# Gates fetched to half of the partitions and copied to the other half by ScalarE

## The chip, the core and the metric

The kernel runs on one core of a Trainium2 chip. A core has five engines with a queue of instructions each: TensorE (PE in the profile, its weight loads PEld), VectorE (DVE), ScalarE (ACT), GpSimd (POOL) and SyncE (SP), which here only issues DMAs. Each engine works through its queue in order, and engines wait for one another and for DMAs by semaphores. The metric is the device time of one execution in microseconds; the figure to compare with is the median of the runs.

## What is computed

The input x is 2 images of 128 channels and 256 x 256 pixels. One layer follows: window attention with a halo (on the four pixel parities apart, because of a fixed mask) after a normalization over channels, and then a mixture of experts in which each pixel takes the two best of eight experts. Cut to what matters:

```python
x = x + attention(_ln_c(x), W_qkv, W_out, rel_height, rel_width)
t = _to_tokens(x)                                   # one token per pixel, 128 channels
h = _ln_t(t)
router_probs = softmax(h @ router_w + router_b)     # 8 experts
top_p, top_i = top_k(router_probs, 2)
top_p = top_p / sum(top_p)
expert_out = einsum('bnd,edc->bnec', h, expert_w) + expert_b
t = t + einsum('bnk,bnkc->bnc', top_p, expert_out[top_i])
```

All of it is in float32.

## The kernel before

**Tiles and loops.** Channels lie on the 128 partitions. The image is cut into 64 strips of 8 pixel rows (32 per image). Each strip has four planes, one for each parity of pixel row and column, so the main loop (L980) runs over 256 planes n. In one pass it does the attention of plane n, the projections (queries, keys, values, relative positions) of plane n + 1, the statistics and the routing of earlier row pairs, and the experts of a row pair (512 tokens: 128 channels x 512) of the strip before.

**Order.** The order within a pass is written out by hand (`manual_schedule`, L979): each generator (`scores`, `attend`, `out_project`, `project`, `norms`, `route`) is moved on by `next(...)` at the place where its instructions shall stand in the queues of all engines. TensorE's order in a usual plane is: scores (L437, L454), values and projections of the next plane (L310, L369, L383, L408), four expert products of the row pair before (L677, experts 4, 6, 7, 5), sums and attended values (L475, L485), statistics (L543), expert products 0, 1, 2, the output projection (L513), expert product 3.

**Gates.** A row pair goes through these steps, spread over three planes:
1. `norms` squares the rows on ScalarE (L537), sums over channels on TensorE (L543), transposes on VectorE (L552) and makes the rate 1/sqrt(variance) in `rstd`: VectorE L192 to L195, then Ln and Exp on ScalarE (L196, L197), then VectorE L198, L199, L559, L561.
2. In the next plane `route` (L576 to L608) picks the two best experts on VectorE, with an Exp on ScalarE (L581). `spread` transposes the gates (L614) and writes them to a DRAM buffer gd (L622).
3. In the same plane they are read back, each of them as one row of 512 numbers that is repeated on all 128 partitions: the rate rb for the attention's normalization (`fetch_rstd`, L628), the mean term sb (`fetch_means`, L657) and the eight gates gb (`fetch`, L652). `to_all` (L631) builds the repeated source. A gate's buffer is one of eight; a write of a single column by VectorE (L651) or ScalarE (L649) just ahead of the DMA marks the place in the order from which the DMA may start.
4. In the plane after that, `means` (L662) adds the mean term and `times` (L668) multiplies the rows by each gate, experts 0 to 4 and 6 on VectorE, 5 and 7 on GpSimd; `product` (L677) multiplies by the expert's weights, and `end` (L683) adds the sum to the rows, which are then stored (L715). `ln1` (L236, GpSimd) applies rb.

**SyncE's queue.** In a usual plane it issues, in this order: gates 5 and 7, gd twice, the value rows to DRAM (vrows, L329), rb, sb, the value windows from DRAM (vwin twice, L341, which need the value rows landed), gates 0, 1, 2, the load of x (L117), gate 3, the store (L715), gates 4 and 6.

**Blocks of instructions.** TensorE's instructions are fetched in blocks of 256. `addr_align` pads its stream so that what follows stands at a given slot of a block: once at the start (L101), at the start of each usual plane (L995, slot 157), and in planes without a normalization ahead (plane 6 and planes 250 to 255) before the sums (L1027, slot `SUMS_AT`).

**The end.** `finish_last` (L722) handles the last row pairs: those called row B here (the `nxt` of the loop's end, L793) and then five more, one of which (f) is routed first and the last four in one pass over VectorE (L798 to L849). Their gates are fetched whole (L745, L747), multiplied in `multiply` (L760, two of eight on GpSimd in the first four) and summed in `products` (L767) into the four quarters of one PSUM tile, accs; L878 and L882 add.

Of the kernel before, what the change touches and what calls it, by code (L numbers as in the profile page):

```python
# [11 lines left out]
F32 = mybir.dt.float32  # L12
AF = mybir.ActivationFunctionType
ALU = mybir.AluOpType
# [3 lines left out]
P = 128  # L18
HEADS, DH = 4, 32
E = 8  # L20
# [23 lines left out]
KR, KC = 6, 10  # L44
NK = KR * KC
SLOT = 64
BLOCK, FIRST_LIMIT, SUMS_AT = 256, 99, 40
NU = 9
FILL = 6

# [2 lines left out]
def kernel(  # L53
# [16 lines left out]
    nc = tc.nc  # L70
# [7 lines left out]
    CH = 2 * W  # L78
    NT = CH // P
# [13 lines left out]
    def mm_tile(name):  # L93
        return ps_mm.tile([P, 512], F32, tag="mm", name=name)

    def ctile(shape, name):
        return const.tile(shape, F32, tag=name, name=name)


    nc.scalar.preload_act_table_set("natural_log_exp_and_others")  # L100
    nc.tensor.addr_align(BLOCK, offset=51, max_nops=0)  # L101


    strips = [(b, s) for b in range(B) for s in range(NS)]
# [27 lines left out]
    rb = ctile([P, E], "rb")  # L132
    ew = ctile([P, E, P], "ew")
# [491 lines left out]
    def fetch_rstd(gd, nm):  # L625

        rb = gates.tile([P, NT * P], F32, tag="rb", name=f"rb{nm}", bufs=2)
        nc.sync.dma_start(rb, to_all(gd, E + 1))  # L628
        return rb

    def to_all(gd, j):  # L631

        return gd[j * NT : (j + 1) * NT].rearrange("r k -> (r k)").partition_broadcast(P)

    class Experts:

# [6 lines left out]
        def fetch(self, e, eng):  # L643


            nm = "_".join(str(v) for v in (*self.at, e))
            self.gb[e] = gates.tile([P, NT * P], F32, tag="gb", name=f"gb{nm}", bufs=8)
            if eng is nc.scalar:
                eng.copy(self.gb[e][:, 0:1], onesm[:, 0:1])  # L649
            else:  # L650
                eng.memset(self.gb[e][:, 0:1], 0.0)  # L651
            nc.sync.dma_start(self.gb[e], to_all(self.gd, e))  # L652

        def fetch_means(self):

            self.sb = gates.tile([P, NT * P], F32, tag="sb", name="sb%d_%d" % self.at, bufs=1)
            nc.sync.dma_start(self.sb, to_all(self.gd, E))  # L657

        def means(self):

# [24 lines left out]

    class NoExperts:
        def fetch(self, e, eng):
            pass

        def fetch_means(self):  # L690
# [31 lines left out]
    def finish_last(ex, nxt, gated):  # L722
# [27 lines left out]
        def multiply(at, row):  # L750

            sb, gb = rooms.pop(0)
            src = rows_of(*at)
            xs = work.tile([P, CH], F32, tag="o", name=f"xl{row}")
            nc.vector.tensor_add(xs, src, sb)
            out = []
            for e in range(E):
                xe = work.tile([P, CH], F32, tag="xe", name=f"xel{row}_{e}", bufs=8)
                eng = nc.gpsimd if e in (2, 5) and row < 4 else nc.vector
                eng.tensor_tensor(xe, xs, gb[e], ALU.mult)  # L760
                out.append(xe)
            return out

        def products(acc, xes):
            order = (0, 1, 3, 2, 4, 6, 5, 7)
            for j, e in enumerate(order):
                nc.tensor.matmul(  # L767
                    acc, lhsT=ew[:, e, :], rhs=xes[e], start=(j == 0), stop=(j == E - 1)
                )

        gd = spread(f, None, made[0], "_c")
# [18 lines left out]
        nxt.means()  # L790
        ex.end()
        for e in (0, 1, 2, 3, 4, 6, 5, 7):
            nxt.times(e, nc.gpsimd)  # L793
        for e in (0, 1, 2, 3, 4, 6, 5, 7):
            nxt.product(e)

# [66 lines left out]
            2, gds[1], [gates.tile([P, CH], F32, tag="gb", name=f"gl2_{e}", bufs=8) for e in range(E)]  # L863
        )

        accs = ps_att.tile([P, 4, CH], F32, tag="att", name="accs")
        todo = [f] + rows
        before = nxt
        for row, at in enumerate(todo):
            xes = multiply(at, row)  # L870
            if row < 2:
                fetch_all(row + 3, gds[row + 2])
            if row == 0:
                before.end()
                store(*to_store.pop())
            else:
                src = rows_of(*todo[row - 1])
                nc.vector.tensor_add(src, accs[:, (row - 1) % 4], src)  # L878
                store(*todo[row - 1])
            products(accs[:, row % 4], xes)  # L880
        src = rows_of(*todo[-1])
        nc.vector.tensor_add(src, accs[:, (len(todo) - 1) % 4], src)  # L882
        store(*todo[-1])

    n_planes = 4 * len(strips)
# [1 line left out]
    def row_at(n):  # L887

        i, pl = divmod(n + 2, 4)
        for j, k in ((i + 1, pl + 2), (i + 2, pl - 2)):
            if 0 < j < len(strips) and k in ln_rows(j) and (k > 1 or strips[j][1] == 0):
                return j, k
        return None
# [77 lines left out]
    none = iter(())  # L973
    gated, ex, nxt = None, NoExperts(), NoExperts()
    last = ctile([P, 1], "last")
    pool, dve = nc.gpsimd, nc.vector

    ET = mybir.EngineType
    with tc.manual_schedule(engines={ET.PE, ET.DVE, ET.Activation, ET.Pool, ET.SP}):  # L979
        for n in range(n_planes):  # L980
            i, pl = divmod(n, 4)
            score, attn, outp, ahead, norm, rout = none, none, none, none, none, none
            if n < n_planes:
                score = scores(n, states[n])
                attn = attend(n, states[n])
                outp = out_project(n, states[n])
            if n + 1 < n_planes:
                states[n + 1] = {}
                ahead = project(n + 1, states[n + 1])

            usual = n > 6 and row_at(n - 1) is not None
            if usual:
                nc.tensor.addr_align(BLOCK, offset=BLOCK - FIRST_LIMIT)  # L995


            next(score, None)
            new, row = NoExperts(), None
            if gated and gated[0]:  # L1000
                rout = route(*gated[0], *gated[2])
            next(rout, None)
            nxt.fetch(5, nc.scalar)
            for _ in rout:
                pass
            next(score, None)
            next(ahead, None)
            nxt.fetch(7, nc.scalar)
            if gated:
                f, c, made = gated  # L1010
                gd = spread(f, c, made[0], f"_{n}")
                new = Experts(*f, gd) if f else new
            if n + 1 < n_planes:
                send_values(n + 1, states[n + 1]["sent"])
            if gated and c:
                row = (*c, fetch_rstd(gd, f"_{n}"))
            next(ahead, None)
            if n + 1 < n_planes:
                states[n + 1]["shift"]()
            filling = n < FILL  # L1020
            if not filling:
                next(ahead, None)
                next(ahead, None)
            for e in (4, 6, 7, 5):
                ex.product(e)
            if n >= 6 and not usual:
                nc.tensor.addr_align(BLOCK, offset=SUMS_AT)  # L1027


            f = (i - 1, pl) if 0 < i <= len(strips) else None  # L1030
            c = row_at(n)
            if f or c:
                room = None
                if filling:
                    room = ps_acc.tile([P, 512], F32, tag="acc", name=f"plt_{n}")
                norm = norms(f, c, f"_{n}", room)
            next(norm, None)
            next(attn, None)
            nxt.means()
            new.fetch_means()  # L1040
            if n + 1 < n_planes:
                take_values(n + 1)
            for e in (0, 1, 2, 3):
                nxt.times(e, dve)
            new.fetch(0, dve)
            for e in (4, 6):
                nxt.times(e, dve)
            new.fetch(1, dve)
            ex.end()
            new.fetch(2, dve)  # L1050
            next(attn, None)
            next(attn, None)


            ex = nxt
            next(norm, None)
            if filling:
                next(ahead, None)
                next(ahead, None)
            load_x((n + 9) // 4, (n + 9) % 4, paced=True)  # L1060
            new.fetch(3, dve)
            while to_store:
                store(*to_store.pop())
            next(ahead, None)
            ex.product(0)
            made = next(norm, None)
            ex.product(1)
            ex.product(2)
            new.fetch(4, nc.scalar)
            nxt.behind(6)  # L1070
            nxt.times(5, pool)
            if row:
                ln1(*row, pool)
            if pl == 3 and i + 2 < len(strips):
                halo(i + 2)
            nxt.times(7, pool)
            if n + 2 < n_planes:
                borders(n + 2)
            next(outp, None)
            ex.product(3)  # L1080
            next(outp, None)
            new.fetch(6, dve)
            gated, nxt = (f, c, made) if made else None, new
            states.pop(n, None)

        finish_last(ex, nxt, gated)
# [59 lines left out]
```

## Time and profile before

| | |
|---|---|
| three runs | 4287.52, 4296.25, 4299.03 us (median 4296.25) |
| the profiled execution | 4302.19 us, its span 4300.4 us |
| mean granted clock of TensorE | 0.994 |
| moved by DMA | 1022 MB, of it 12.6 MB instructions in 769 packets |
| share of the 16 DMA engines, data queue | 75.7% |
| gates fetched | 2008 DMAs of 256 KB, 5.7 us to landing (median) |
| value windows fetched | 512 DMAs of 240 KB, 4.8 us |
| expert products L677 | 4016 TensorE matmuls, 1880.8 us |
| products by gates L668 | VectorE 1500, 685 ns each; GpSimd 508, 1272 ns each |
| usual plane, start to start | 16.25 us |
| from the last plane's start to the end | 92.4 us |

How to read it: the profile gives each engine's busy time and, for each group of instructions, the line, the engine, the operation, the tiles (out<-in), the shape and the count; then the busy time, the mean time of one and the idle time of the engine ahead of it with what ended that idle time. SPq marks DMA issues by SyncE; a DMA's time to landing runs from its issue to its semaphore. In a timeline line the first number is the start and the second the length, in microseconds, of the instructions merged into that line.

### The profile page before, as it was taken

To read this page: it belongs to the slowest core of one execution; us is meant where nothing else is said; L and a number is where in the kernel's file an instruction comes from. 1 tells how busy PE (TensorE), PEld (TensorE's weight loads), DVE (VectorE), ACT (ScalarE), POOL (GpSimd) and SP (SyncE) were. 2 spreads that over 40 slices of the span, in tenths; PEclk is the share of its full clock that TensorE was granted. 3 is DMA by queue.
4 is the path that set the end of the run, shared out by engine and by line. 5 is a ranking of instruction groups with operands and counts; after the bars stand their busy time and mean duration, and the time that the engine had idled before them with its cause. 6 is when DMAs were issued, how large, how long until landed. Compare 5 with 4: busy or idle time off the path is not lost.

```text
span 4300.4 us, 224047 instructions
## 1 busy us (share of the span) xinstructions
PE 4214.7 (98%) x94273; PEld 2457.6 (57%) x94273; DVE 3786.3 (88%) x11752; ACT 1315.5 (31%) x3750; POOL 1093.2 (25%) x1125
## 2 busy tenths in 40 slices
PE   7999999999999999999999999999999999999997
PEld 5555555555555555555555555555555555555553
DVE  5888898998988888998898888989898888888887
ACT  3333333332323232333333333323233333333320
POOL 1222222222222222222222222222222222222222
PEclk9999999999999999999999999999999999999999
DMA  4777777877787877887778787787778787777776
GB/s 141 228 248 238 245 242 244 244 245 243 240 248 233 251 235 234 247 244 242 247 239 249 237 249 239 246 245 244 238 243 249 234 249 238 243 234 247 232 217 198
DMA packets 824576, 1022.15 MB, mean 238 GB/s; under 512 B 137634, under 2 KB 409634, under 8 KB 823594
## 3 DMA queue, kind: packets, MB, share of 16 engines
q1 hardware_dynamic: 822864, 1007.52, 75.7%
q8 instruction: 769, 12.60, 1.3%
q14 instruction: 213, 1.74, 0.1%
q10 hardware_dynamic: 730, 0.29, 0.0%
HBM read 863.78 MB, written 143.75 MB: 234 GB/s over the span
## 4 chain that ended last, share of the span: by engine, by line
PE 97%; issue 1%; DVE 1%; DMA 1%; SPq 0%; ACT 0%; POOL 0%; POOLq 0%; DVEq 0%
PE acc L677 41%; PE att L454 8%; PE att L485 7%; PE pv L310 7%; PE plt L543 6%; PE pu L369 5%; PE po L513 5%; PE pk L383 5%; PE pq L408 5%; PE att L437 4%; PE att L475 3%; DMA gl<-gd_l 1%; PE accs L767 0%; PE pltn L253 0%; DMA xt<-in_x_dram 0%
## 5 line engine op out<-in xcount | busy, mean ns | idle before, releaser
L677 PE MATMUL acc<-xe,ew 128*128 128x512 f32 x4016 | 1880.8, 599 | 10.2 <-issue 8.9
L677 PEld LDWEIGHTS acc<-xe,ew 128*128 128x128 f32 x4016 | 740.9, 190 | 913.0 <-issue 856.3
L668 DVE TENSOR_TENSOR xe<-xs,gb 128x512 f32<-128x512 f32 x1500 | 927.6, 685 | 8.6
L672 POOL COPY last<-xe 128x1 f32<-128x1 f32 x250 | 45.9, 184 | 3042.7 <-DVE gb L651 3042.7
L668 POOL TENSOR_TENSOR xe<-xs,gb 128x512 f32<-128x512 f32 x508 | 645.4, 1272 | 12.2 <-DMA gb<-gd 10.7
L454 PE MATMUL att<-qs,kcol 32*60 32x32 f32 x32768 | 393.9, 222 | 25.2 <-issue 24.7
L454 PEld LDWEIGHTS att<-qs,kcol 32*60 32x60 f32 x32768 | 388.1, 126 | 29.7 <-issue 29.0
L236 POOL TENSOR_TENSOR xn<-xt,rb 128x512 f32<-128x512 f32 x249 | 374.4, 1504 | 87.5 <-DMA rb<-gd 74.2
L485 PEld LDWEIGHTS att<-pT,vwin 64*32 64x32 f32 x32768 | 350.8, 105 | 48.6 <-issue 11.1
L485 PE MATMUL att<-pT,vwin 64*32 64x32 f32 x32768 | 348.7, 201 | 9.1 <-issue 8.4
L462 ACT ACTIVATE pT<-att 128x1024 f32<-128x1024 f32 x256 | 262.0, 1023 | 269.4 <-PE att L454 269.3
L310 PE MATMUL pv<-wt,xn 128*128 128x128 f32 x2048 | 300.3, 290 | 0.0
L537 ACT ACTIVATE sq<-xt 128x512 f32<-128x512 f32 x501 | 290.2, 630 | 0.0
L357 DVE STREAM_TRANSPOSE au<-auT 128x512 f32<-128x512 f32 x256 | 269.5, 1053 | 8.8
L373 DVE STREAM_TRANSPOSE uT<-pu 128x512 f32<-128x512 f32 x256 | 183.2, 716 | 105.2 <-PE pu L369 102.1
L394 ACT COPY kcol<-pk 128x560 f32<-128x560 f32 (+2 forms) x344 | 183.0, 532 | 290.5 <-PE pk L383 287.7
L513 PE MATMUL po<-o,wt 128*128 128x512 f32 x512 | 262.1, 593 | 4.5 <-ACT kcol L404 2.1
L369 PE MATMUL pu<-xn,wrel 128*128 128x512 f32 x512 | 266.0, 601 | 0.0
L408 PE MATMUL pq<-xn,wt 128*128 128x512 f32 x512 | 261.8, 592 | 1.6 <-issue 1.6
L383 PE MATMUL pk<-xn,wt 128*128 128x512 f32 (+2 forms) x528 | 262.4, 580 | 0.0
L310 PEld LDWEIGHTS pv<-wt,xn 128*128 128x128 f32 x2048 | 251.0, 193 | 10.6 <-DVE xn L236 0.2
L437 PEld LDWEIGHTS att<-au,keys 32*64 32x64 f32 x8192 | 116.0, 131 | 195.5 <-PE po L513 189.2
(2445 smaller groups left out, 4935.1 us busy)
## 6 DMA issues: line engine op xcount, KB each, us to landing
gb<-gd SPq DMA_DIRECT2D x2008, 256.0 KB, 5.7
vwin<-vrows SPq DMA_DIRECT2D x512, 240.0 KB, 4.8
xt<-in_x_dram SPq DMA_DIRECT2D x256, 256.0 KB, 6.6
out_dram<-xt SPq DMA_DIRECT2D x256, 256.0 KB, 6.0
sb<-gd SPq DMA_DIRECT2D x251, 256.0 KB, 4.3
rb<-gd SPq DMA_DIRECT2D x249, 256.0 KB, 3.5
vrows<-vr SPq DMA_DIRECT2D x168, 256.0 KB, 3.9
vrows<-vr SPq DMA_DIRECT2D x160, 128.0 KB, 3.4
```

The lines of the kernel that those rows point to most:

```text
L236: eng.tensor_tensor(xn[i % 2][:, :, :, k, 1 : PC + 1], ln1_src(i, k).rearrange("p (y j x) -> p y x j", y=2, x=2), rb.rearrange("p (y j x) ...
L310: nc.tensor.matmul(pv[:, j * P : (j + 1) * P], lhsT=xp[:, k, 1 : PC + 1], rhs=wv, start=True, stop=True,)
L369: nc.tensor.matmul(pu, lhsT=wrel, rhs=inner, start=True, stop=True)
L383: nc.tensor.matmul(pk[:, : m * PC], lhsT=wk, rhs=xp[:, part[0] : part[0] + m, 1 : PC + 1], start=True, stop=True,)
L408: nc.tensor.matmul(pq, lhsT=wq, rhs=inner, start=True, stop=True)
L437: nc.tensor.matmul(sc[rows, h].rearrange("p (t w z) -> p t w z", w=2, z=16)[:, :, w], lhsT=keys[hp, turn, w], rhs=au[hp, half * NP + w : ( ...
L454: nc.tensor.matmul(sc[rows, h, 32 * t : 32 * t + 32], lhsT=kk[hp, half * HP + t, 0:NK], rhs=qs[hp, m0 : m0 + 2].rearrange("p m a s -> p (m ...
L485: nc.tensor.matmul(av[hp, half, 32 * t : 32 * t + 32], lhsT=vv[rows, t, hp], rhs=pT[rows, h, 32 * t : 32 * t + 32], start=True, stop=True,)
L513: nc.tensor.matmul(po, lhsT=wo, rhs=state["o"].rearrange("p f z -> p (f z)"), start=True, stop=True)
L537: nc.scalar.activation(sq, src, AF.Square)
L668: eng.tensor_tensor(self.xe[e], self.xs, self.gb.pop(e), ALU.mult)
L677: nc.tensor.matmul(self.acc, lhsT=ew[:, e, :], rhs=self.xe.pop(e), start=(e == 0), stop=not self.xe)
```

## The change

Gates, means and rates are fetched to partitions 0 to 63 alone (`fetch_half`). ScalarE copies them to partitions 64 to 127 (`other_half`, called by `double`, `double_means` and for the rates directly). The copies stand at these places of ScalarE's queue: gate 3 after the values' copy of the next plane, gates 4, 6 and 5 after the projections' copies, then, behind a copy of one column that waits for the attended values (`behind_values`), the rates, the means, gate 7 and the new gate 0, all ahead of the Ln of `norms`; and gates 1 and 2 after its Exp and after the mark of gate 4. The slots of two alignments change. In `finish_last` row B's products and all products of the five later row pairs go to VectorE in expert order, and each later row pair has a PSUM tile of its own from the pool of three. The places of the DMA issues in SyncE's queue stay.

```diff
-BLOCK, FIRST_LIMIT, SUMS_AT = 256, 99, 40
+BLOCK, FIRST_LIMIT, SUMS_AT = 256, 99, 9
...
-    nc.tensor.addr_align(BLOCK, offset=51, max_nops=0)
+    nc.tensor.addr_align(BLOCK, offset=23, max_nops=0)
...
-        nc.sync.dma_start(rb, to_all(gd, E + 1))
+        fetch_half(rb, gd, E + 1)
...
+    def fetch_half(tile_, gd, j):
+        nc.sync.dma_start(tile_[0:SLOT], to_all(gd, j, SLOT))
+    def other_half(tile_):
+        nc.scalar.copy(tile_[SLOT:], tile_[0:SLOT])
...
-            nc.sync.dma_start(self.gb[e], to_all(self.gd, e))
+            fetch_half(self.gb[e], self.gd, e)
+        def double(self, e):
+            other_half(self.gb[e])
...
-                eng = nc.gpsimd if e in (2, 5) and row < 4 else nc.vector
-                eng.tensor_tensor(xe, xs, gb[e], ALU.mult)
+                nc.vector.tensor_tensor(xe, xs, gb[e], ALU.mult)
...
         for e in (0, 1, 2, 3, 4, 6, 5, 7):
-            nxt.times(e, nc.gpsimd)
+            if e > 2:
+                nxt.double(e)
+            nxt.times(e, nc.vector)
...
-        accs = ps_att.tile([P, 4, CH], F32, tag="att", name="accs")
+        accs = []
...
-            products(accs[:, row % 4], xes)
+            accs.append(mm_tile(f"accl{row}"))
+            products(accs[row], xes)
...
             nxt.fetch(7, nc.scalar)
+            nxt.double(3)
...
             c = row_at(n)
+            for e in (4, 6, 5):
+                nxt.double(e)
...
             new.fetch(3, dve)
+            nc.scalar.copy(behind_values, states[n]["att"][:, 1, 511:512])
+            if row:
+                other_half(row[2])
+            new.double_means()
+            nxt.double(7)
+            new.double(0)
...
             made = next(norm, None)
             ex.product(1)
             ex.product(2)
             new.fetch(4, nc.scalar)
+            new.double(1)
+            new.double(2)
```

## The prediction

> **What bounds the kernel now.** I read the engine shares first, then the chain of work that ended last.
>
> ```profile
> PE 4214.7 (98%) x94273; PEld 2457.6 (57%) x94273; DVE 3786.3 (88%) x11752; ACT 1315.5 (31%) x3750; POOL 1093.2 (25%) x1125
> ...
> PE 97%; issue 1%; DVE 1%; DMA 1%; SPq 0%; ACT 0%; POOL 0%; POOLq 0%; DVEq 0%
> ```
>
> TensorE is the bound, and VectorE at 88% is close behind; ScalarE has room. In the timeline a plane starts with the first matmul of L437. Plane 8 starts at 139.58 us and plane 250 at 4124.05, so 242 planes take 3984.5 us; the usual plane is 16.246, and 242 of those are 3931.5. So 53 us are lost in the loop. The waits of TensorE between 300 and 4100 us say where:
>
> ```profile
> PE att L454 <- issue: 16.7, 29, 1.4
> PE acc L677 <- issue: 8.9, 20, 0.8
> ```
>
> L485 adds 3.3. No engine releases these. In the timeline they sit after the 98th, 354th and 610th of a plane's 736 TensorE instructions, 256 apart, where a 16 KB packet of the instruction queue brings the next block. Nothing else holds TensorE in the loop: a gain there can only come out of these 53 us.
>
> Next, one plane of the timeline, from ScalarE's Ln (L196) to the Ln of the plane after it at 2029.03:
>
> ```profile
> 2012.78 0.18 ACT L196 ACTIVATE r__121_38773<-plg 128x8 f32<-128x8 f32 x1 [7.12 <-DVE plg L195]
> ...
> 2018.01 0.24 DVE L614 STREAM_TRANSPOSE gT<-g 128x64 f32<-128x64 f32 x1
> ```
>
> and of the same plane what SyncE issues:
>
> ```profile
> 2018.73 1.45 SPq L622 DMA_DIRECT2D gd<-gT  x2
> 2020.23 0.58 SPq L329 DMA_DIRECT2D vrows<-vr  x1
> ...
> 2023.92 0.91 SPq L341 DMA_DIRECT2D vwin<-vrows  x2
> 2024.93 1.44 SPq L652 DMA_DIRECT2D gb<-gd  x3
> ```
>
> The reader is to see an order: Ln, VectorE's routing, the gates written to DRAM (gd), the value rows written (vrows), read back as windows (vwin), and only then the first gate (gb 0) asked for. The tile view of gb for that first issue says when it lands:
>
> ```profile
> DMA to landing us min/median/max: 7.0/7.0/7.0
> ```
>
> So gb 0 lands at 2024.93 + 7.0 = 2031.9, that is 2.9 us after the next Ln wants to start. Now nobody minds, since the gate is used a plane later.
>
> **The change, part by part.**
>
> Fetches. Ten tiles a plane (eight gates, means, rates) are fetched to 64 partitions: 1.28 MB less of 1007.5 MB / 256 planes = 3.94 MB a plane. SP issues as many DMAs, in the same order.
>
> ScalarE gets ten copies of 64x512 and one 128x1 a plane. No such row exists; the nearest are a copy of 128x512 at 588 ns (L410) and a Square of 128x512 at 630 (L537). With 570: 10 x 0.57 + 0.18 = 5.9 us on top of 1315.5 / 256 = 5.1, 11 of 16.2. As busy time this is hidden by TensorE. Copies 3, 4, 6 and 5 delay the Squares from about 6.2 to 8 us after the plane's start; their matmuls (L543) come at 10.7, so 1.5 us remain even with the copies. Rates, means and gate 7 fit into the 7.12 us of idle before Ln.
>
> The added wait that matters is `new.double(0)`. It waits for gb 0 and stands on ScalarE's queue ahead of Ln and Exp (L196, L197). Behind these wait VectorE's L198 to L614, then SP's gd, vrows and vwin, and behind vwin the next gb 0. The ring closes once a plane, so its length is a floor for the plane:
> - Ln to the end of gT: 2018.25 - 2012.78 = 5.47, all dependent work of VectorE and ScalarE.
> - gT to gd's issue: 0.48 here, since gb 7 is issued just ahead; with the routing late that is out of the way: 0.05.
> - gd's issue to vrows' issue: 1.22 (4164.85 to 4166.07 below).
> - vrows' issue to gb 0's landing, call it X. In loaded planes it is 2031.9 - 2020.23 = 11.7; the median over planes is 11.1 (5.70 to 16.79 us after the plane's start). The last planes load no x and no rates:
>
> ```profile
> 4164.85 1.17 SPq L622 DMA_DIRECT2D gd<-gT  x2
> 4166.07 0.58 SPq L329 DMA_DIRECT2D vrows<-vr  x1
> ...
> 4170.50 0.39 SPq L652 DMA_DIRECT2D gb<-gd  x1
> ```
>
> with gb 0 landing 4.8 us after its issue: X = 9.2; the other such planes give 9.5 to 9.7. With halved gates the load lies between. I take 9.5, nearer to the light rows since halved traffic and a longer plane both thin the queue; bounds 8.6 (9.2 less 0.6, one gate's spacing in landing) and 11.1.
> - wake and copy: 0.65.
>
> Sum: 5.47 + 0.05 + 1.22 + 9.5 + 0.65 = 16.89 us, with bounds 16.0 and 18.5. Over 16.25 the ring sets the plane, and the 53 us of late blocks vanish inside it: 242 x 16.89 - 3984.5 = +102.9. Planes 251 to 254, now 15.42, 15.83, 15.71 and 15.87 long, go to 16.89 as well: +4.7.
>
> Does half the partitions mean half the transfer time? The windows view of two stretches at the start, where first one vwin transfer (60 partitions) runs alone and then both halves run together:
>
> ```profile
> 37.40:38.20 0.80, 0.80 (x5) 0.45 (x4) 0.75 (x2) 0.06 (x1) 0.00 (x0) 1.00 0.36 97
> 38.30:39.10 0.80, 0.80 (x3) 0.06 (x1) 0.77 (x2) 0.71 (x2) 0.00 (x0) 1.00 1.05 317
> ```
>
> The next to last column is the DMA share, the last GB/s: alone 97 (154 in its steadier slices), together 317. The Trainium skill, "SBUF — State Buffer", section "Door 1: The DMA port swizzle (why [64,N] ≈ [32,N])", gives the reason: partitions 0 to 63 reach 8 of 16 ports, and a 64-partition tile moves no faster than 32. By that rule a halved gate takes as long as a whole one and X stays near 11, a plane of 18.4; by the byte count alone it would save a third of the traffic. The rows side with the rule on rate, yet the upper engines become free for the second vwin, so I stay at 9.5.
>
> Alignment. L101 moves 51 to 23, SUMS_AT 40 to 9. The start (planes 0 to 6) has some 16 us of block waits whose places move: 0, bounds -5 and +5. At plane 250 the padding before L475 falls from 94 to 63 slots; its wait was 1.82, so 31 x 1.82 / 94 = 0.6, and up to 4 if the half-clock stretch after it goes: -1.
>
> Tail.
>
> ```profile
> 4230.03 9.87 POOL L668 TENSOR_TENSOR xe<-xs,gb 128x512 f32<-128x512 f32 x8 [10.72 <-DMA gb<-gd]
> ...
> 4280.87 7.13 PE L767 MATMUL accs<-xel,ew 128*128 128x512 f32 x16 [1.49 <-DVE xt L878]
> ```
>
> Row B's eight products move to VectorE ahead of the last routing: 8 x 0.61 = 4.9 later. In exchange POOL no longer runs beside it: L808, L811 to L813, L820 and L822 took 0.98, 0.69, 1.19, 1.19, 0.98, 0.92 where rows of the same sizes take 0.17 to 0.29, 4.7 us in all. Net 0. Separate accumulators take away L767's waits for L878, 4.23 + 3 x 1.4 = 8.6; VectorE then has 0.67 + 8 x 0.61 + 0.68 = 6.2 a row, under TensorE's 16 x 0.43 = 6.9. I take -8, bounds -13 and +2.
>
> Sum on the profiled execution (4302.2; its span is 4300.4): +102.9 + 4.7 - 1 - 8 = +98.6, 4400.8. That execution lies 5.9 over the median of 4296.25, so 4395.
>
> **Rivals.**
>
> A, the ring stays under 16.25. It needs X of at most 8.9. For it: one vwin without load landed 3.1 us after issue, its pair 3.6, and gb 0 would follow only the lower half's queue. Against it: X was 9.2 to 9.7 with hardly any other traffic. Then TensorE sets the plane and the change pays what it can: a third of the bytes gone would save 18 of the 53 us, all gone 53; half is 27. With tail and padding -36: 4302 - 36 - 6 = 4260. This is the faster side.
>
> B, the ring is long enough to cool TensorE. The windows view after one wait of 1.43 us at L454 (ended at 1653.1) has, third from the end, a granted clock of 0.51:
>
> ```profile
> 1654.80:1658.30 3.50, 3.50 (x10) 2.04 (x9) 0.53 (x1) 1.37 (x3) 0.00 (x0) 0.51 0.19 69
> ```
>
>  If X is 10.5 or more, the plane is 17.9 and TensorE idles 1.6 us in each; from about 1.4 us of idle on, such a stretch of 3.4 us at half clock costs 1.7 us of matmul again, so it cannot catch up. 242 x 17.9 - 3984.5 = +347: 4640. The page "TensorE: Matmul & The Clock Gate", section "What's actually happening", has the same 3.4 us window. For B: the loaded median of 11.1. Against: the halved bytes.
>
> C, it comes out even: a ring of 16.45 to 16.55 gives back in the loop what the tail gains, 4296 within 13.
>
> **How the numbers follow.** Forecast (ring 16.55 to 17.45) 0.53, A 0.33, B 0.08, C 0.06. The likeliest case gives 4395, its own range is 4310 to 4530 (242 x 16.55 and 242 x 17.45 in the same sum). The range that takes in A and C is 4245 to 4530; B and the ends of the others are left out. About 0.3%, 13 us, is what a measurement of this kernel can tell from no change: faster 0.33, same 0.06, slower 0.61.
>
> **What would show it.** Right: ScalarE's L196 starts right after a copy that waited for DMA gb; VectorE waits at L198 for ScalarE by some 2 us a plane instead of 0.5; TensorE waits at L513 or its weight load for VectorE; planes are 16.9 long and even, with no block waits left. Wrong in favour of A: gb 0 lands within 14 us of the plane's start, L196 still waits for VectorE, planes are 16.25 and fewer block waits remain. B shows as a granted clock well under 0.99 in every slice. For the tail, L767 without waits for the additions, and 84 us from the last L437 on instead of 92.

## The result, and the profile after

| | before | after |
|---|---|---|
| median of four runs | 4293.85 us (4287.52 to 4299.03) | 4540.36 us (4533.59 to 4544.31) |
| ratio | | 1.0576 (95% interval 1.0557 to 1.0596) |
| span of the profiled execution | 4300.4 us | 4531.8 us |
| planes 8 to 249, first L437 of 8 to first L437 of 250 | 3984.5 us | 4210.1 us (+225.6) |
| usual plane (median); mean of the 242 | 16.25; 16.46 us | 17.28; 17.40 us |
| start to plane 8 | 139.6 us | 144.1 us (+4.6) |
| planes 250 to 254 | 83.9 us | 94.6 us (+10.6) |
| from the last plane's start | 92.4 us | 83.0 us (-9.4) |

The four differences sum to 231.4 us, the difference of the spans. Nearly all of it is the loop. The page of the changed kernel: first the engine shares, then the data queue (packets, MB, share of 16 engines), the chain that ended last, and two groups of ScalarE (busy time, mean ns | idle before them and what ended it).

```profile
PE 4257.8 (94%) x94273; PEld 2474.0 (55%) x94273; DVE 3752.5 (83%) x11768; ACT 2729.8 (60%) x6514; POOL 1079.8 (24%) x1109
...
q1 hardware_dynamic: 662352, 678.79, 55.1%
...
DVE 53%; issue 17%; ACT 13%; PE 8%; DMA 8%; SPq 1%; DVEq 0%; ACTq 0%
...
L641 ACT COPY gb<-gb 64x512 f32<-64x512 f32 x2008 | 1145.0, 614 | 46.3 <-DMA gb<-gd 27.2
...
L1089 ACT COPY behind_values<-att 128x1 f32<-128x1 f32 x256 | 40.8, 159 | 1367.7 <-DVE gb L659 1367.7
```

TensorE held 97% of the chain before and holds 8% now; VectorE and ScalarE hold 66%. The data queue fell from 75.7% to 55.1%, so the change did thin the traffic. But ScalarE stood 1367.7 us in front of the one-column copy L1089, 5.5 us a plane, while all copies of gates together waited 27.2 us for DMAs. The list of waits says who stood behind ScalarE (total, times, longest):

```profile
ACT behind_values L1089 <- DVE gb L659: 1367.7, 250, 8.8
...
POOL xn L236 <- ACT rb L641: 620.6, 230, 30.3
...
PEld att L437 <- ACT gb L641: 259.0, 240, 1.4
...
ACT gb L641 <- DMA gb<-gd: 27.2, 36, 4.7
```

So at most 36 of some 250 copies of gate 0 waited for their DMA (that line counts the copies of all gates). One plane of the timeline shows what sets its length:

```profile
2129.59 0.17 DVE L198 SCALAR_TENSOR_TENSOR plg<-plg,r__121_40063 128x8 f32<-128x8 f32 x1 [1.86 <-ACT r__121_40063 L197]
...
2138.72 1.34 PE L485 MATMUL att<-pT,vwin 64*32 64x32 f32 x128
...
2143.26 0.69 DVE L505 TENSOR_TENSOR o<-att,rT 128x512 f32<-128x512 f32 x1
...
2144.03 0.16 ACT L1089 COPY behind_values<-att 128x1 f32<-128x1 f32 x1 [5.58 <-DVE gb L659]
...
2144.22 0.62 ACT L641 COPY rb<-rb 64x512 f32<-64x512 f32 x1
...
2144.74 0.61 ACT L641 COPY sb<-sb 64x512 f32<-64x512 f32 x1
...
2145.26 1.13 ACT L641 COPY gb<-gb 64x512 f32<-64x512 f32 x2
...
2146.42 0.18 ACT L196 ACTIVATE r__122_40391<-plg 128x8 f32<-128x8 f32 x1
2146.63 0.21 ACT L197 ACTIVATE r__122_40391<-r__122_40391 128x8 f32<-128x8 f32 x1
...
2146.87 0.17 DVE L198 SCALAR_TENSOR_TENSOR plg<-plg,r__122_40391 128x8 f32<-128x8 f32 x1 [1.86 <-ACT r__122_40391 L197]
```

The values' matmuls (L485) are done at 2140.06, yet L1089 starts at 2144.03. It starts 0.09 us after VectorE's L505 ends: over all 256 planes 0.087 to 0.088 us behind L505 from the 5th to the 95th percentile, and 3.98 us (median) behind L485. The list names the gate mark L659, a one-column write of VectorE that ends at about the same time, but the order of the signals in the trace rules it out. ScalarE's semaphore instruction ahead of the copy starts 0.057 us before it (median of planes 8 to 249; at least 0.056). L505's signal comes 0.077 us before the copy, L659's only 0.054 us before (at most 0.055), when that instruction has already begun. L1089 and L505 both read the tile `att`, in the same bank of PSUM. So there is a ring that the prediction does not have: VectorE from L198 to the end of L505 takes 14.35 us (median; in the plane above no gap between its instructions is over 0.035 us), and from there over L1089, four copies (in a row each starts 0.52 us after the one before), Ln and Exp back to L198 it is 2.92 us. Together 17.27, the usual plane.

The Trainium skill has the rule: "PSUM — Partial Sum Buffer", section "PSUM bank collisions raise a hardware error", says that accesses of two different engines to one bank and quadrant have to be ordered by software, reads against reads too. The trace agrees: one read starts 0.088 us after the end of the other.

### The profile page after: what moved, and what is told of

It reads as the page before. It is cut to its first block, busy times and chain, and to the rows that moved or that the text cites. A ratio compares the mean times of both kernels' runs of the same rounds, so it can differ in the third digit from the quotient of the medians.

```text
span 4531.8 us, 226178 instructions
## 1 busy us (share of the span) xinstructions
PE 4257.8 (94%) x94273; PEld 2474.0 (55%) x94273; DVE 3752.5 (83%) x11768; ACT 2729.8 (60%) x6514; POOL 1079.8 (24%) x1109
## 3 DMA queue, kind: packets, MB, share of 16 engines
q1 hardware_dynamic: 662352, 678.79, 55.1%
## 4 chain that ended last, share of the span: by engine, by line
DVE 53%; issue 17%; ACT 13%; PE 8%; DMA 8%; SPq 1%; DVEq 0%; ACTq 0%
DVE xe L684 11%; DMA gb<-gd 6%; ACT gb L641 5%; DVE sT L495 3%; DVE rT L500 3%; DVE xt L518 3%; DVE o L505 3%; DVE xs L678 3%; PE acc L693 3%; ACT rb L641 3%; DVE uT L373 3%; ACT sb L641 2%; DVE cmp L590 2%; DVE cmp L596 2%; DVE rank L600 2%
## 5 line engine op out<-in xcount | busy, mean ns | idle before, releaser
L641 ACT COPY gb<-gb 64x512 f32<-64x512 f32 x2008 | 1145.0, 614 | 46.3 <-DMA gb<-gd 27.2
L1089 ACT COPY behind_values<-att 128x1 f32<-128x1 f32 x256 | 40.8, 159 | 1367.7 <-DVE gb L659 1367.7
L684 POOL TENSOR_TENSOR xe<-xs,gb 128x512 f32<-128x512 f32 x500 | 635.1, 1270 | 28.9 <-ACT gb L641 28.2
L454 PE MATMUL att<-qs,kcol 32*60 32x32 f32 x32768 | 408.6, 222 | 3.6 <-issue 3.6
L454 PEld LDWEIGHTS att<-qs,kcol 32*60 32x60 f32 x32768 | 407.0, 126 | 4.0 <-issue 4.0
L485 PEld LDWEIGHTS att<-pT,vwin 64*32 64x32 f32 x32768 | 354.0, 105 | 51.8 <-issue 14.2
L485 PE MATMUL att<-pT,vwin 64*32 64x32 f32 x32768 | 350.6, 200 | 15.9 <-issue 15.9
L537 ACT ACTIVATE sq<-xt 128x512 f32<-128x512 f32 x501 | 288.9, 623 | 6.1
L437 PEld LDWEIGHTS att<-au,keys 32*64 32x64 f32 x8192 | 123.6, 131 | 272.6 <-ACT gb L641 259.0
```

Of the source, the lines that this page charges most:

```text
L454: nc.tensor.matmul(sc[rows, h, 32 * t : 32 * t + 32], lhsT=kk[hp, half * HP + t, 0:NK], rhs=qs[hp, m0 : m0 + 2].rearrange("p m a s -> p (m ...
L485: nc.tensor.matmul(av[hp, half, 32 * t : 32 * t + 32], lhsT=vv[rows, t, hp], rhs=pT[rows, h, 32 * t : 32 * t + 32], start=True, stop=True,)
L537: nc.scalar.activation(sq, src, AF.Square)
L641: nc.scalar.copy(tile_[SLOT:], tile_[0:SLOT])
L684: eng.tensor_tensor(self.xe[e], self.xs, self.gb.pop(e), ALU.mult)
```

## The experiments

All kernels below compute the whole reference. Those of one group ran on one chip beside the kernel before, and ratios are against those runs. "Loop" is planes 8 to 249 of the profiled execution; chips differ there (tail_only, whose loop is that of before, has 3967.7 us, 17 less), so medians and loops of different groups are compared by their ratios.

| kernel | median us | ratio (95% interval) | loop us | mean plane | planes 250 to 254 |
|---|---|---|---|---|---|
| no_mark | 4522.28 | 1.0506 (1.0489 to 1.0523) | 4194.8 | 17.33 | 100.9 |
| gate0_late | 4432.28 | 1.0289 (1.0271 to 1.0307) | 4104.6 | 16.96 | 97.9 |
| no_mark_gate0_late | 4358.93 | 1.0124 (1.0106 to 1.0142) | 4029.6 | 16.65 | 100.2 |
| old_slots | 4547.15 | 1.0561 (1.0545 to 1.0576) | 4219.7 | 17.44 | 88.7 |
| gates_next | 4284.47 | 0.9998 (0.9987 to 1.0009) | 3961.2 | 16.37 | 101.3 |
| gates_next_slots | 4263.23 | 0.9950 (0.9934 to 0.9966) | 3963.9 | 16.38 | 81.1 |
| whole_no_mark | 4670.75 | 1.0900 (1.0875 to 1.0926) | 4339.8 | 17.93 | 104.0 |
| tail_only | 4273.79 | 0.9972 (0.9961 to 0.9982) | 3967.7 | 16.40 | 85.9 |
| mark_early | 4459.51 | 1.0421 (1.0400 to 1.0441) | 4140.6 | 17.11 | 98.3 |
| mark_next_slots | 4397.58 | 1.0274 (1.0256 to 1.0291) | 4090.8 | 16.90 | 84.7 |
| whole_next_slots | 4268.08 | 0.9977 (0.9965 to 0.9989) | 3969.2 | 16.40 | 85.1 |

In the expectations, S is the theory that L1089's wait for L505 sets the plane, and P that the prediction's ring through gate 0's landing does.

**no_mark.** The changed kernel without the one-column copy.

```diff
-            nc.scalar.copy(behind_values, states[n]["att"][:, 1, 511:512])
```

> The changed kernel without the one-column copy behind_values (L1089). Theory S: in the changed kernel this copy waits for VectorE's L505, which ends 14.8 us after the plane's start, so four copies of 0.53 us stand between L505 and the Ln of L196; from L505 to L198 it is 2.83 us, VectorE's work from L198 to L505 is 14.45, and the ring is 17.28. Without the mark, rates, means and gate 7 are copied in ScalarE's idle time before VectorE asks for Ln, and Ln waits at most for gate 0, issued at 10.6: a plane of 16.25 to 16.4, 4270 to 4320 us. Theory P (the prediction's): the ring goes through gate 0's landing and is 16.9 however the mark stands: 4420 to 4450 us.

S missed: the time is 4522, not 4270 to 4320. P has the mechanism, but its ring is longer than it expected (4420 to 4450). In ScalarE's timeline the rates are copied early, and then gate 0's copy waits for its DMA, with Ln right behind it:

```profile
2116.68 0.62 ACT L641 COPY rb<-rb 64x512 f32<-64x512 f32 x1 [2.33 <-DMA rb<-gd]
...
2122.43 0.62 ACT L641 COPY gb<-gb 64x512 f32<-64x512 f32 x1 [3.60 <-DMA gb<-gd]
2123.07 0.18 ACT L196 ACTIVATE r__121_39941<-plg 128x8 f32<-128x8 f32 x1
```

Over the whole run 220 copies of gates waited for their DMA here, where the changed kernel has 36. So there are two rings of nearly equal length, and taking one away leaves the other.

**gate0_late** and **no_mark_gate0_late.** Gate 0 is copied after Exp, beside gates 1 and 2; the second kernel leaves out the one-column copy as well.

```diff
-            new.double(0)
...
+            new.double(0)
             new.double(1)
             new.double(2)
```

> The changed kernel with new.double(0) moved behind Ln and Exp, next to double(1); the mark stays. Theory S: one copy of 0.53 us fewer stands between L505 and Ln, so a plane of 16.75 and 4540 - 128 = 4412 us. Theory P: nothing ahead of Ln waits for gate 0 any more, so a plane of 16.25 and 4260 to 4300 us.

> Both edits: no mark, and new.double(0) behind Ln and Exp. Both theories: no ring, TensorE sets the plane at 16.25, 4260 to 4300 us. The sum of planes 8 to 249 over 242 x 16.246 = 3931.5 then shows what halved gate traffic does to the waits for instruction blocks, 53 us before: 18 if they go by the packets moved, 53 if the half fetch takes as long as a whole one.

With the one-column copy kept and gate 0 late the usual plane is 16.78, the ring of 17.28 less one copy of 0.52: S holds, P's 4260 to 4300 does not. Without both the time should have come back to that of before, and 1.2% stayed. ScalarE's timeline of that kernel shows what is late next:

```profile
2115.42 0.18 ACT L196 ACTIVATE r__126_41580<-plg 128x8 f32<-128x8 f32 x1 [1.60 <-DVE plg L195]
...
2116.68 1.79 ACT L641 COPY gb<-gb 64x512 f32<-64x512 f32 x3 [0.76 <-DMA gb<-gd]
2118.49 0.23 ACT L581 ACTIVATE lg<-lg 128x32 f32<-128x32 f32 x1
```

Ln now waits for VectorE alone, as before the change. But the three copies behind it wait for gates 0 to 2, and the route's Exp (L581) stands behind them: it starts 0.56 us (median) after L580 where it took 0.03 before. In the list of waits VectorE is the one that pays:

```profile
DVE cmp L590 <- ACT lg L581: 159.5, 162, 2.8
```

**old_slots.** The changed kernel with the alignments of before.

```diff
-BLOCK, FIRST_LIMIT, SUMS_AT = 256, 99, 9
+BLOCK, FIRST_LIMIT, SUMS_AT = 256, 99, 40
...
-    nc.tensor.addr_align(BLOCK, offset=23, max_nops=0)
+    nc.tensor.addr_align(BLOCK, offset=51, max_nops=0)
```

> The changed kernel with the alignments of before (51 and SUMS_AT 40 in place of 23 and 9). If slot 9 is what makes planes 251 to 254 as long as 21.1, 17.0, 17.9 and 20.9 us (waits of 1.4 to 3.7 us inside L485), they fall to about 17.3 and the time by 8 to 15 us, 4525 to 4532. If the ring or the clock makes them, it stays at 4540.

The medians lie on different chips; the ratios, 1.0561 and 1.0576 for the changed kernel, overlap in their intervals. The time alone would say "not the slots", and that reading is too quick: in the profiled executions planes 250 to 254 are 5.9 us shorter than in the changed kernel and the end 2.6, while a single wait of 17.0 us at the first matmul of plane 7, which no engine releases, takes it back at the start. Whether the other runs have that wait is not known.

**gates_next** and **gates_next_slots.** No one-column copy; gate 0 is copied a plane later with gate 3, gates 1 and 2 with 4 and 6, gate 5 behind the Squares, so that no copy stands ahead of Ln or of the route's Exp that waits for a late DMA. The second kernel has the sums of planes 250 to 255 at slot 40.

```diff
             nxt.double(3)
+            nxt.double(0)
...
-            for e in (4, 6, 5):
+            for e in (1, 2, 4, 6):
                 nxt.double(e)
...
             next(norm, None)
+            nxt.double(5)
...
-                nc.tensor.addr_align(BLOCK, offset=SUMS_AT)
+                nc.tensor.addr_align(BLOCK, offset=SUMS_AT if n == 6 else 40)
```

> After without the one-column copy behind the attended values, and with gates 0, 1 and 2 copied one plane later (gate 0 with gate 3, gates 1 and 2 with 4 and 6, gate 5 behind the Squares). All of the computation is there. Theory E: in no_mark_gate0_late the 45 us left in the loop come from the route's Exp (L581), which stood 0.56 us (median) behind the copies of gates 0 to 2 while VectorE waited 159 us for it at L590. Then L581 follows L580 after 0.03 us again, planes 8 to 249 take 3985 us or less (down to 3935 if the late instruction blocks stay away as they did there), and the time is before +16 (planes 250 to 254) -9 (tail) +0 to -50: 45 under to 10 over before. Rival L: ScalarE's ten copies or the moved DMAs slow the loop wherever they stand; then planes stay near 16.46 and the time about 52 over before.

> gates_next with the sums of planes 250 to 255 at slot 40 again (plane 6 keeps slot 9). Theory: the waits of 1.4 to 3.8 us for nothing that the profile shows, inside L485 in planes 250 to 255, come from slot 9 and go; 8 to 14 us under gates_next. Rival: they come from the transfers' state at the end and stay; within 4 us of gates_next.

Theory E holds: L581 follows L580 after 0.03 us again and the loop is 6 us under that of tail_only on the same chip. What was left over before sits in planes 250 to 254 (+15.4 against tail_only), and slot 40 takes 20 of it away. TensorE's waits between 4105 and 4215 us, first of gates_next:

```profile
PE att L485 <- issue: 16.2, 6, 3.7
PE att L475 <- issue: 3.1, 1, 3.1
```

and of gates_next_slots, where L485 is gone from the list:

```profile
PE att L475 <- ACT gb L641: 3.0, 1, 3.0
PE att L475 <- issue: 1.8, 1, 1.8
```

The six waits at L485 in gates_next, 1.1 to 3.7 us long, end 1.3 to 1.6 us after a packet of the instruction queue has arrived: they are waits for instruction blocks. So slot 9 is at fault in the late planes: 21 us between the two medians. In the changed kernel it costs less, 5.9 us by old_slots; that its longer planes hide a part was not tested. gates_next_slots is the fastest kernel of the study, 0.5% under before. Its shares and chain:

```profile
PE 4219.3 (99%) x94273; PEld 2476.9 (58%) x94273; DVE 3798.1 (89%) x11768; ACT 2762.2 (65%) x6258; POOL 1078.1 (25%) x1109
...
PE 98%; DMA 1%; DVE 1%; ACT 0%; issue 0%; SPq 0%; DVEq 0%; ACTq 0%
```

ScalarE is as busy as in the changed kernel, and TensorE is the bound again. The ten copies cost time by their places, not by their work.

**tail_only.** The kernel before with the edits of `finish_last`.

```diff
-                eng = nc.gpsimd if e in (2, 5) and row < 4 else nc.vector
-                eng.tensor_tensor(xe, xs, gb[e], ALU.mult)
+                nc.vector.tensor_tensor(xe, xs, gb[e], ALU.mult)
...
-            products(accs[:, row % 4], xes)
+            accs.append(mm_tile(f"accl{row}"))
+            products(accs[row], xes)
```

> The kernel before with the change's edits of the end alone (row B's and the later rows' products on VectorE in expert order, a PSUM tile for each later row). All of the computation is there. Theory: from the last plane's start to the end 83 to 84 us instead of 92.4, so 8 to 9.5 us under before. Rival: the 9.4 us that the changed kernel's end gained came from shorter fetches; then within 3 us of before.

From the last plane's start it is 81.8 us against 92.4, and the time by the ratio 0.28% under before (interval 0.18 to 0.39), some 12 us. The end's gain belongs to these edits.

**mark_early.** The one-column copy is kept, but written ahead of VectorE's reads of `att`. Then nothing of VectorE is before it in the order of the bank, and it waits for L485 alone, which is what the prediction took it to do.

```diff
+        nc.scalar.copy(behind_values, att[:, 1, 511:512])
         sT = work.tile([P, 2, HQ], F32, tag="sT", name=f"sT{n}", bufs=1)
...
-            nc.scalar.copy(behind_values, states[n]["att"][:, 1, 511:512])
```

> After, with the one-column copy written ahead of VectorE's work on the attended values (L495 to L505) instead of behind it, so that it waits for TensorE's L485 alone, as the prediction took it to do. Theory M (the copy cost what it cost by waiting for VectorE's L505, and gate 0's landing alone makes the ring that the prediction summed): the time is that of no_mark within 10 us, 4.8 to 5.3% over before; L196 follows a copy that waited for DMA gb; the plane is 17.33 on average. Rival (a copy that waits for L485 holds up ScalarE's queue wherever it stands): as after, 5.8% over before or more.

The ratio is 1.0421: the loss is smaller than M's 4.8 to 5.3%, and far from the rival's 5.8%. ScalarE's timeline has the order that the prediction described (the file has a line more, so numbers behind L494 are one higher):

```profile
2122.97 0.16 ACT L494 COPY behind_values<-att 128x1 f32<-128x1 f32 x1 [1.75 <-PE att L485]
...
2123.25 0.62 ACT L642 COPY rb<-rb 64x512 f32<-64x512 f32 x1
...
2128.07 0.62 ACT L642 COPY gb<-gb 64x512 f32<-64x512 f32 x1 [3.17 <-DMA gb<-gd]
2128.72 0.18 ACT L196 ACTIVATE r__123_40721<-plg 128x8 f32<-128x8 f32 x1
```

The same copy, 0.16 us of work, costs 1.5% more when it stands behind L505 (1.0576 less 1.0421). The edit has a small price of its own: VectorE's L496, which reads `att` next, stood 26.6 us in all behind the copy, 46 times. Why the ring is 0.22 us shorter than in no_mark is not settled; between the value rows' issue and gate 0's copy it is 0.30 us shorter.

**mark_next_slots.** gates_next_slots with the one-column copy at the change's place, ahead of the rates, the means and gate 7.

> gates_next_slots with the one-column copy back at its place in the change, ahead of the rates, the means and gate 7. Theory M: the chain from VectorE's L198 to the end of L505 (14.45 us in after) is closed by L505's end, the copy of 0.16, three copies of 0.52, Ln and Exp to a ring of 16.75 us as in gate0_late, over the 16.37 of gates_next_slots: 242 x 0.38 = 92 us over gates_next_slots, 1.6% over before. Rival (the ring needs a copy that waits for a DMA too): within 15 us of gates_next_slots.

It lies 3.2% over gates_next_slots by the ratios, 139 us, where 92 were expected: the mechanism is right and the size was off. ScalarE stood 903.6 us in front of the one-column copy, and no wait for a DMA is needed for that: none of its copies waited for one here. The expectation set the planes at 16.75; their mean is 16.90, and gates_next_slots' was 16.38: 242 x 0.52 = 126.

**whole_no_mark** and **whole_next_slots.** no_mark and gates_next_slots, with every tile fetched to all 128 partitions; the copies stay.

```diff
-        nc.sync.dma_start(tile_[0:SLOT], to_all(gd, j, SLOT))
+        nc.sync.dma_start(tile_, to_all(gd, j))
```

> no_mark, but every tile is fetched to all 128 partitions as before (the copies stay and write the same numbers once more). Theory R: a fetch to 64 partitions takes as long as one to 128, so the time from the value rows' issue to gate 0's landing stays at 9.5 us (median in no_mark), the plane at 17.1, the time within 40 us of no_mark's 4522. Theory B: halving made it shorter; then it is near the 11.1 of before, planes are some 18.7 and the time about 4522 + 242 x 1.6 = 4910.

> gates_next_slots, but every tile is fetched to all 128 partitions again (the copies stay and write the same numbers once more). Theory H (the halved fetches thin the traffic that delays the blocks of instructions): the block waits at the 98th, 354th and 610th instruction of a plane come back to 35 to 50 us in the loop and the time lies 25 to 45 us over gates_next_slots, at or over before. Rival (the copies' order or the program's layout took the waits away): within 8 us of gates_next_slots.

In whole_no_mark, value rows' issue to gate 0's copy takes 10.39 us on average against 9.77 in no_mark, and gate 0's issue to its copy 6.35 against 5.52: with all ten tiles halved a gate is there 13% sooner, neither R's nothing nor B's 1.6 us. The Trainium skill, "SBUF — State Buffer", section "Door 1: The DMA port swizzle (why [64,N] ≈ [32,N])", lets a 64-partition tile gain no rate over 32, so that the halved gate would take as long as the whole one; the 13% stand against taking that to the letter in a loaded queue.

In whole_next_slots the waits for instruction blocks come back, as TensorE's waits between 300 and 4100 us show:

```profile
PE att L454 <- issue: 9.7, 22, 1.5
PE acc L693 <- issue: 5.7, 13, 1.1
PE att L485 <- issue: 3.0, 10, 0.4
```

while gates_next_slots has one line in the same stretch:

```profile
PE att L437 <- issue: 0.2, 1, 0.2
```

With the weight loads' waits this is over 30 us after the 98th, 354th and 610th instruction; in gates_next_slots it is under 1 us. Theory H has its mechanism, but not its size: the time was to rise by 25 to 45 us. But the usual plane is 16.24 with whole fetches and 16.35 with halved ones, for a reason not found, and this takes most of it back: 0.27% remain between the two kernels, with intervals that touch.

## Why the prediction was wrong

- **The step that failed**: "Rates, means and gate 7 fit into the 7.12 us of idle before Ln", with the one-column copy counted as 0.18 us of ScalarE's time alone. It was taken to wait for TensorE's values, which are done 10.9 us into the plane; it waits for VectorE's L505, which ends at 14.8. Then three copies, and gate 0's as a fourth, stand between VectorE's last work on `att` and Ln, and close a second ring of 17.28 us. mark_early shows the loop with the assumption true (+156 us, on another chip; ratio 1.0421), the changed kernel without it (+226; 1.0576).
- **The ring through gate 0** is there behind the other one, and was under-sized (+102.9 us predicted for the loop). The terms, as predicted, and then as measured on average in mark_early and no_mark: Ln to gd's issue 5.52 | 5.59 | 5.56; gd to the value rows 1.22 | 1.35 | 1.34; X 9.5 | 9.47 | 9.77; copy and wake 0.65 | 0.70 | 0.67. Sum 16.89 | 17.11 | 17.33. The term in dispute, X, was right in mark_early and 0.27 short in no_mark; the others were read from one plane each, and small excesses of 0.05 to 0.13 add up over 242 planes (in mark_early 0.22 x 242 = 53 us). The usual plane of mark_early, 16.86, is the predicted one, but its planes are not even: every second one is longer, 17.5 against 16.5 us (medians). Why is open.
- **Planes 250 to 254**: +3.7 predicted, +10.6 measured. The padding was costed as a small gain; slot 9 brings block waits inside L485. With slot 40 (old_slots) it is +4.8.
- **Start**: 0, bounds 5; +4.6. **Tail**: -8; -9.4, and L787 no longer waits for the additions. TensorE's timeline of the changed kernel:

```profile
4489.32 15.96 PE L787 MATMUL accl<-xel,ew 128*128 128x512 f32 x32 [8.39 <-DVE xel L781]
4507.05 20.87 PE L787 MATMUL accl<-xel,ew 128*128 128x512 f32 x48 [1.77 <-DVE xel L781]
```

- **Copies**: 0.57 us each predicted, 0.614 in the profile; as busy time they were hidden, as said.
- **Rival A** (TensorE keeps the plane, a third to all of the block waits go) is what gates_next does: block waits gone, but with a loop only 6 us under tail_only's. **Rival B** (cooling) did not come: the granted clock is 0.995 with 0.9 us of idle in a plane. Nor does it follow from the length of the plane: whole_no_mark has B's planes, 17.9 us with 1.25 us of idle in several waits, and a clock of 0.994. A single wait of 1.4 us does not decide it either, as the prediction took it: whole_no_mark has one of 1.55 us with no stretch at half clock behind it, and the kernel before has one of 1.14 us with such a stretch. **C** did not come.
- **Signs to look for**: VectorE's wait at L198 came as forecast (1.86 us), and so did the vanished block waits, but by another ring. The sign that told the two apart was the first one, "L196 starts right after a copy that waited for DMA gb": true of 36 planes at most.

## What to carry to other kernels

A wait added to an in-order queue is worth what its latest releaser makes of it: list every engine that touches the same PSUM bank ahead of it, reads included, and place it ahead of those that it does not need. Then follow the queue behind it around the loop, and look for a second ring nearly as long as the first, for taking one away leaves the other. Copies are cheap on an engine with 70% idle as long as none stands ahead of a short instruction that a busy engine needs while it waits itself, for a late DMA (no_mark) or behind a late wait for another engine (mark_next_slots, where no copy waits for a DMA).

## What the hardware did that was not expected

- A ScalarE copy of 64x512 takes 614 ns, no less than 128x512 (588 ns at L410 before): on half of the partitions it takes no less time. L410 reads PSUM; a Square of 128x512 from SBUF takes 623 ns (L537, changed kernel).
- Where the sums stand within a block of 256 instructions is worth 20 us in six planes: slot 9 against 40, by waits of up to 3.7 us that no engine releases and that end 1.3 to 1.6 us after a packet of the instruction queue.
- One wait that no engine releases, in old_slots, lasted 17.0 us. The last packet of the instruction queue had come 9.0 us before its end, so it is not of the kind above. Why is open.
